# Another order of ScalarE's and VectorE's work inside a four-slot round of a fused decoder layer

## The chip, the core and the metric

The kernel runs on one NeuronCore of a Trainium2 chip. The metric is the device time of one execution in microseconds. The engines named below are TensorE (PE, with PEld for its weight loads), VectorE (DVE), ScalarE (ACT), GpSimd (POOL) and SyncE (SP, which only issues DMAs).

## The reference

One decoder layer with normalisation behind each residual, for 32 sequences of 256 tokens with 256 features:

```
x = layernorm(x + self_attention(x))
x = layernorm(x + cross_attention(x, ctx, cell))
x = layernorm(x + feed_forward(x))
```

- Self attention: 16 query heads of 64, 4 key/value heads, rotary positions, a linear position bias per head, a full softmax over 256 keys, output projection.
- Cross attention: layer norms with weights ahead of the q, k, v and output projections, 16 heads of 16, windows of 64 queries that look at their own and the previous window of keys, a mask by cell number, rotary positions.
- Feed forward: inner size 1024, `silu(gate) * up`, with weights rounded to -1, 0, 1 times a scale and activations rounded to 8 bits per row.

Inputs and outputs are float32; only the feed-forward products run in bfloat16, where the rounded values are exact.

## The kernel before

All 32 sequences ("batches") run in one unrolled program that is software-pipelined by hand. Time is cut into **slots**; a sequence takes 16 slots, four **rounds** of four slots (`part` 0 to 3). In round `m` the self attention works on pair `m` of units (a unit is 128 queries and two query heads per key/value head of a pair, 512 columns per tile), and the cross attention on unit `k = m - 4`, that is on the sequence before. The document calls the four rounds of a sequence A (slots 0 to 3), B (4 to 7), C (8 to 11) and D (12 to 15).

The order of instructions on TensorE, VectorE and ScalarE is the order in which the Python code calls them (`manual_schedule`). GpSimd and SyncE are not in that set: their instructions are ordered by the tile framework's planner, by its own estimate of when each becomes ready, and then run strictly in that order.

What one round does, by function and line:

- `self_scores` (line 393 on TensorE, 409 on VectorE): 8 matmuls into two banks `s`; then four VectorE instructions add the position bias, write `p` and give the negated row maximum `nm`. Two such units per round.
- `self_exp` (427, ScalarE): for each unit and half, two exponentials with their row sums.
- `self_values` (487 TensorE, 494 ScalarE): the previous pair's `pT` times `v` gives `o`; ScalarE copies it to `oT`. `self_normal` (500, VectorE) multiplies `oT` with `R`, the reciprocal sums.
- `cross_turn` (708 TensorE, 710 ScalarE): transposes the previous cross unit's exponentials `xp` and copies them to `xpT`, in two halves.
- `cross_scores` (669 TensorE, 683 VectorE), `cross_values` (724 TensorE, `xo`; 733 ScalarE, `xoT`), `cross_exp` (699 ScalarE, four exponentials per half).
- `self_inverse` (441, 443 VectorE, then a transposing DMA `planes`), and `self_spread` (455, GpSimd), which makes `R` of it.
- `self_turn` (470 TensorE, 475 ScalarE): transposes a unit's `p` and copies it to `pT`, two copies per unit.
- `cross_back` (744 TensorE, 749 and 750 VectorE): transposes the cross output back and divides it by its sums.

Between these, `parts()` runs the next step of every generator that is due in the slot: projections (`self_inputs`, 330, 339, 346; `cross_inputs`, 617, 629), output projections and norms (`self_output`, `cross_output`), and the feed forward. A generator's `yield n` says in how many slots it goes on. For example `self_output` starts in slot 9 (and 17): two steps of `wo` matmuls (508), the deferred normalisation (below) in slot 11 (19), the transposes `zqT` (204) with their copy `zT` (205, ScalarE) in slot 12 (20), and the `xq` matmuls (545) in slot 14 (22). Counted within a sequence's period of 16, the `zqT` steps fall into part 0 of rounds D and B. The other generators that run in part 0 have no ScalarE instruction in `parts()`.

A few instructions are deferred. A generator appends them to the list `last`, and `flush()` issues them at the end of the slot. Such are the normalisations `scaled` (198, ScalarE), and `residual` of `self_output`:

```
nc.vector.tensor_scalar(zq, h, mv[:, 0:1], rs[:, 1:2], ALU.subtract, ALU.mult)
nc.scalar.activation(x1, h, AF.Identity, bias=rs[:, 2:3], scale=rs[:, 0:1])
nc.gpsimd.tensor_tensor(x1, x1, xbias[O_], ALU.add)
```

What is appended in part 3: in slot 3 a `residual`; in slot 7 the two `scaled` of the context `cs`; in slot 11 another `residual`, the second `scaled` of the feed forward's output `y`, and the output DMA (194); in slot 15 nothing.

All TensorE outputs go through one pool of eight PSUM banks (`bank`, tag "b"), so a matmul group may wait until the engine that reads an older bank is done.

Of the kernel before, what the change touches and what calls it, by code (L numbers as in the profile page):

```python
# [51 lines left out]
def kernel(  # L52
# [139 lines left out]
    def flush():  # L192
        while last:
            last.pop(0)()
# [700 lines left out]
    with tc.manual_schedule(engines={mybir.EngineType.PE, mybir.EngineType.DVE, mybir.EngineType.Activation}):  # L895
        running = []
        slot = min(starts)
        while starts or running:
            m, part = divmod(slot, 4)
            k = m - CROSS  # L900
            for gen in starts.pop(slot, ()):
                running.append([slot, gen])

            def cross(f, unit, *more):
                if 0 <= unit < 4 * B:
                    f(*divmod(unit, 4), *more)

            def pair(f, unit):
                if 0 <= unit < 4 * B:
                    f(*divmod(unit, 4))  # L910

            def own(f, unit, *more):
                if 0 <= unit < 8 * B:
                    f(*divmod(unit, 8), *more)

            def parts():
                for r in list(running):
                    if r[0] == slot:
                        wait = next(r[1], r)
                        if wait is r:  # L920
                            running.remove(r)
                        else:
                            r[0] += wait or 1

            if part == 0:
                own(self_scores, 2 * m)
                own(self_scores, 2 * m + 1)
                own(self_exp, 2 * m, 0)
                own(self_exp, 2 * m, 1)
                own(self_exp, 2 * m + 1, 0)  # L930
                pair(self_values, m - 1)
                cross(cross_turn, k - 1, 0)
                cross(cross_turn, k - 1, 1)
                own(self_exp, 2 * m + 1, 1)
                parts()
                pair(self_normal, m - 1)
            elif part == 1:
                parts()
                cross(cross_scores, k)
                cross(cross_values, k - 1)  # L940
                cross(cross_exp, k, 0)
            elif part == 2:
                parts()
                pair(self_inverse, m)
                cross(cross_exp, k, 1)
                own(self_turn, 2 * m)
                cross(cross_back, k - 1)
            else:
                own(self_turn, 2 * m + 1)
                parts()  # L950
                pair(self_spread, m)
            flush()
            slot += 1

# [86 lines left out]
```

## Time and profile before

| | |
|---|---|
| median of 3 runs | 2209.35 us (2208.95 to 2211.95) |
| profiled execution | 2211.08 us, span of its trace 2209.3 us |
| mean granted TensorE clock | 0.98 |
| busy share PE, PEld | 95%, 73% |
| busy share DVE, ACT, POOL | 81%, 75%, 60% |
| DMA | 177.59 MB, mean 80 GB/s |

A profile line of a group reads: line, engine, operation, tiles written and read, count, busy time, mean duration in ns, idle time of the engine ahead of it and what ended that. A line of the list of waits reads: who waited, for whom, us in total, how many times, and the longest. A line of the timeline reads: start and duration in us, engine, line, operation, tiles, shapes, count, and in brackets the engine's idle time ahead of it with its releaser. A line of the windows reads: from and to, length, then busy time (and instruction count) of PE, PEld, DVE, ACT and POOL, the granted clock, DMA share and GB/s. The ends of matmuls are modelled, so the start-to-start distance of groups is the safer measure of TensorE.

### The profile page before, as it was taken

What the parts mean: (1) busy time and instruction counts of PE and PEld (TensorE: products, weight loads), DVE (VectorE), ACT (ScalarE), POOL (GpSimd) and SP (SyncE); (2) the same over time, 40 slices, a digit from 0 to 9 for tenths busy, and PEclk for the clock granted to TensorE, in tenths of its full rate; (3) what the DMA queues carried; (4) which work ended last, traced back from release to release, by engine and by line L of the source; (5) the groups of instructions that cost most, each with busy time, mean ns of one, the idle gap of its engine ahead of it and who ended that gap; (6) DMA issues with size and microseconds to landing.
All of it is one profiled execution on the core that took longest, in us unless ns stands there. A gap on an engine that the chain in (4) does not pass through costs nothing.

```text
span 2209.3 us, 54605 instructions
## 1 busy us (share of the span) xinstructions
PE 2103.3 (95%) x17254; PEld 1617.7 (73%) x17316; DVE 1789.9 (81%) x6949; ACT 1659.5 (75%) x4961; POOL 1316.8 (60%) x1977
## 2 busy tenths in 40 slices
PE   7899999999999999999999999999999999999984
PEld 5677777777777777777777777777777777777662
DVE  3877888888888888888888888888888888888775
ACT  2578778787778787778777778877777877777862
POOL 4465655666665666655656655656666556666542
PEclk8999999999999999999999999999999999999985
DMA  6433333333333334333333333334333333333221
GB/s 213 113 78 71 82 78 76 75 78 85 84 79 73 79 74 86 88 76 75 78 74 90 83 75 74 80 74 89 84 79 77 78 73 83 85 78 74 43 52 31
DMA packets 326592, 177.59 MB, mean 80 GB/s; under 512 B 242976, under 2 KB 296096, under 8 KB 326304
## 3 DMA queue, kind: packets, MB, share of 16 engines
q1 hardware_dynamic: 324608, 170.52, 34.1%
q10 hardware_dynamic: 1696, 3.57, 0.4%
q8 instruction: 138, 2.26, 0.4%
q14 instruction: 150, 1.23, 0.2%
HBM read 39.50 MB, written 8.39 MB: 22 GB/s over the span
## 4 chain that ended last, share of the span: by engine, by line
PE 58%; DVE 20%; ACT 12%; DMA 3%; issue 2%; POOL 1%; SPq 0%; ACTq 0%; POOLq 0%; DVEq 0%
PE wo L508 9%; PE t L470 8%; DVE p L409 7%; PE s L393 6%; ACT p L427 6%; PE o L487 5%; PE proj L330 5%; PE ff L811 4%; PE xq L545 3%; PE xt L708 3%; ACT xpT L710 3%; PE ffo L858 3%; PE xk L617 2%; PE xw L770 2%; PE v L362 2%; DMA out_dram<-x 2%
## 5 line engine op out<-in xcount | busy, mean ns | idle before, releaser
L427 ACT ACTIVATE p<-p,nm 128x256 f32<-128x256 f32 x1024 | 508.3, 499 | 235.8 <-DVE nm L409 235.8
L409 DVE CUSTOM_DVE_ANT_0 p<-s,alibi 128x256 f32<-128x256 f32 x1024 | 361.6, 416 | 3.2 <-PE s L393 3.2
L699 ACT ACTIVATE xp<-xp,xnm 128x128 f32<-128x128 f32 x1024 | 328.6, 401 | 47.0 <-DVE xnm L683 46.8
L393 PE MATMUL s<-kT,qT 64*128 64x256 f32 x2048 | 271.4, 392 | 0.0
L475 ACT COPY pT<-t 128x512 f32<-128x512 f32 x512 | 263.7, 598 | 7.0 <-PE t L470 6.8
L470 PE MATMUL t<-ident,p 128*128 128x128 f32 x2048 | 267.0, 273 | 0.9 <-ACT p L427 0.9
L354 POOL TENSOR_TENSOR qT<-qT,other 128x512 f32<-128x512 f32 x128 | 178.7, 1396 | 137.9 <-DMA other<-psin 113.1
L487 PE MATMUL o<-pT,v 128*64 128x256 f32 x2048 | 249.8, 386 | 0.0
L393 PEld LDWEIGHTS s<-kT,qT 64*128 64x128 f32 x2048 | 197.5, 187 | 68.6 <-issue 16.2
L330 PE MATMUL proj<-xT,wq_sb 128*128 128x256 f32 x1024 | 245.8, 384 | 0.0
L508 PE MATMUL wo<-wo_sb,oT 128*128 128x256 f32 x1024 | 244.1, 381 | 0.4 <-DVE oT L500 0.4
L470 PEld LDWEIGHTS t<-ident,p 128*128 128x128 f32 x2048 | 234.9, 142 | 9.4 <-ACT p L427 2.6
L683 DVE CUSTOM_DVE_ANT_0 xp<-xs,mask 128x128 f32<-128x128 f32 x1024 | 225.5, 284 | 13.2 <-PE xs L669 11.0
L508 PEld LDWEIGHTS wo<-wo_sb,oT 128*128 128x128 f32 x1024 | 192.9, 191 | 29.3 <-DVE oT L500 1.1
L487 PEld LDWEIGHTS o<-pT,v 128*64 128x64 f32 x2048 | 136.4, 137 | 98.1 <-issue 42.3
L330 PEld LDWEIGHTS proj<-xT,wq_sb 128*128 128x128 f32 x1024 | 187.7, 193 | 21.9 <-issue 0.4
L500 DVE TENSOR_TENSOR oT<-oT,R 128x512 f32<-128x512 f32 x128 | 98.0, 765 | 119.8 <-ACT oT L494 110.2
L427 ACT ACTIVATION_READ_ACCUMULATOR p<-p,nm 128x1 f32 x1024 | 194.1, 190 | 0.0
L455 POOL COPY R<-planes 128x1024 uint16<-128x1024 uint16 x128 | 173.5, 1356 | 21.9 <-DMA planes<-wide 21.6
L826 DVE SCALAR_TENSOR_TENSOR gu<-gu,ff 128x512 f32<-128x512 f32 x128 | 82.5, 684 | 100.7 <-ACT gu L825 100.6
L847 POOL TENSOR_SCALAR gu<-gu,ffhup 128x1024 f32<-128x1024 f32 x64 | 73.5, 1149 | 143.9 <-DVE ffhup L843 143.9
L708 PEld LDWEIGHTS xt<-ident,xp 128*128 128x128 f32 x1024 | 112.1, 143 | 49.0 <-issue 36.2
(147 smaller groups left out, 4530.8 us busy)
## 6 DMA issues: line engine op xcount, KB each, us to landing
other<-psin SPq DMA_DIRECT2D x640, 64.0 KB, 2.0
xT<-in_xt_dram SPq DMA_DIRECT2D x32, 256.0 KB, 2.8
xs<-in_x_dram SPq DMA_DIRECT2D x32, 256.0 KB, 2.7
cs<-in_ctx_dram SPq DMA_DIRECT2D x32, 256.0 KB, 2.8
other<-qb SPq DMA_DIRECT2D x64, 128.0 KB, 2.0
kTz<-tr SPq DMA_DIRECT2D x256, 32.0 KB, 2.0
other<-qb SPq DMA_DIRECT2D x128, 64.0 KB, 1.9
out_dram<-x SPq DMA_DIRECT2D x32, 256.0 KB, 2.4
```

The lines of the kernel that those rows point to most:

```text
L330: nc.tensor.matmul(pq[:, c * L : (c + 1) * L], w[:, dc, c * P : (c + 1) * P], xT[:, dc, :], start=(dc == 0), stop=(dc == NDC - 1),)
L354: nc.gpsimd.tensor_tensor(d2, d2, other, ALU.add)
L393: nc.tensor.matmul(banks[half][:, rr * L : (rr + 1) * L], qT[rows_, rr, qc * P : (qc + 1) * P], kT[rows_, kc, :], start=(rr == 0), stop=(r ...
L409: nc.vector.tensor_tensor_reduce(p[:, cols], banks[half][:, cols], alibi[:, 2 * (4 * kc + 2 * rp + rr) + half, :], -0.125, 3.0e38, ALU.add ...
L427: nc.scalar.activation(p[:, cols], p[:, cols], AF.Exp, bias=nm[:, rr : rr + 1], scale=-1.0, accum_out=s["sums", i // 2][:, e : e + 1],)
L470: nc.tensor.transpose(pt[:, j * P : (j + 1) * P], p[half][:, rr * L + kk * P : rr * L + (kk + 1) * P], ident,)
L475: nc.scalar.copy(pT[half], pt)
L487: nc.tensor.matmul(po[half * HD : (half + 1) * HD, rp * L : (rp + 1) * L], s["v"][:, kk, (2 * kc + half) * HD : (2 * kc + half + 1) * HD], ...
L508: nc.tensor.matmul(py[:, 0:D], s["oT", qc, kc][:, r, :], wo_sb[:, 4 * kc + r, :], start=(kc == 0 and r == 0), stop=(kc == 1 and r == 3),)
L683: nc.vector.tensor_tensor_reduce(p[:, cols], banks[2 * half + j // 2][:, j % 2 * P : (j % 2 + 1) * P], s["mask"][:, qc, :], -1.0, 3.0e38, ...
L699: nc.scalar.activation(p[:, cols], p[:, cols], AF.Exp, bias=s["xnm", i][half][:, j : j + 1], scale=-1.0)
L708: nc.tensor.transpose(pt[:, j * P : (j + 1) * P], p[:, j * P : (j + 1) * P], ident)
```

## The change

The diff moves calls inside the round's four parts. In part 0 the second unit's scores are issued behind the first unit's exponentials and a new `flush()`; the generators' steps run ahead of the second unit's last exponentials. The two halves of the cross exponentials move from part 1 and the head of part 2 to behind the first unit's transposes (part 2) and behind the generators' steps of part 3. The `flush()` at the end of part 3 is left out: what part 3 deferred is issued by the flush in the next part 0, or behind the loop for the last slot.

```
             if part == 0:
                 own(self_scores, 2 * m)
-                own(self_scores, 2 * m + 1)
                 own(self_exp, 2 * m, 0)
                 own(self_exp, 2 * m, 1)
+                flush()
+                own(self_scores, 2 * m + 1)
                 own(self_exp, 2 * m + 1, 0)
                 pair(self_values, m - 1)
                 cross(cross_turn, k - 1, 0)
                 cross(cross_turn, k - 1, 1)
+                parts()
                 own(self_exp, 2 * m + 1, 1)
-                parts()
                 pair(self_normal, m - 1)
             elif part == 1:
                 parts()
                 cross(cross_scores, k)
                 cross(cross_values, k - 1)
-                cross(cross_exp, k, 0)
             elif part == 2:
                 parts()
                 pair(self_inverse, m)
-                cross(cross_exp, k, 1)
                 own(self_turn, 2 * m)
+                cross(cross_exp, k, 0)
                 cross(cross_back, k - 1)
             else:
                 own(self_turn, 2 * m + 1)
                 parts()
+                cross(cross_exp, k, 1)
                 pair(self_spread, m)
-            flush()
+            if part < 3:
+                flush()
             slot += 1
+        flush()
```

The order of the calls that issue TensorE instructions stays as it was: `self_scores` of both units, `self_values`, `cross_turn`, the generators.

More of the change, by code (lines that the diff above doesn't have):

```diff
@@ L926 @@
                 own(self_scores, 2 * m)
-                own(self_scores, 2 * m + 1)
                 own(self_exp, 2 * m, 0)
                 own(self_exp, 2 * m, 1)
+                flush()
+                own(self_scores, 2 * m + 1)
                 own(self_exp, 2 * m + 1, 0)
@@ L933 @@
                 cross(cross_turn, k - 1, 1)
+                parts()
                 own(self_exp, 2 * m + 1, 1)
-                parts()
                 pair(self_normal, m - 1)
@@ L940 @@
                 cross(cross_values, k - 1)
-                cross(cross_exp, k, 0)
             elif part == 2:
@@ L944 @@
                 pair(self_inverse, m)
-                cross(cross_exp, k, 1)
                 own(self_turn, 2 * m)
+                cross(cross_exp, k, 0)
                 cross(cross_back, k - 1)
@@ L950 @@
                 parts()
+                cross(cross_exp, k, 1)
                 pair(self_spread, m)
-            flush()
+            if part < 3:
+                flush()
             slot += 1
+        flush()
 def shape_constants():
```

## The prediction

> **What bounds the kernel now.** I read the page first, then the windows, the list of waits, and last the timeline of one batch. Batches repeat every 65.5 to 66 us, so one is enough.
>
> ```profile
> PE 2103.3 (95%) x17254; PEld 1617.7 (73%) x17316; DVE 1789.9 (81%) x6949; ACT 1659.5 (75%) x4961; POOL 1316.8 (60%) x1977
> ```
> ```profile
> 60.00:1000.00 940.00, 914.68 (x7563) 708.53 (x7585) 778.13 (x3018) 728.77 (x2195) 572.13 (x838) 1.00 0.36 81
> ```
>
> The second line is the steady state by window (PE, PEld, DVE, ACT, POOL, clock): TensorE has a matmul in flight for 914.7 of 940 us at full clock. It is the bound, and all that an order of instructions can win is its waits.
>
> Here a rule of the Trainium skill speaks against the change: "Perfetto Trace Analysis", Identifying the Most-Contended Engine, holds matmul occupancy to be no measure of headroom and asks for weight-load occupancy (here 73%), while for VectorE occupancy is fair. By it VectorE (81%) is the most contended, the diff takes none of its 1790 us away, and the sum would be 0. The row I follow is the spacing of matmul starts: `proj` x8 in 1.8 us, `t` x8 in 0.87, with nothing between groups except at four places per batch. Those places lose about 2.4 of 65.8 us, so a perfect order gains 75 us at most, and the rule's 27% isn't there.
>
> ```profile
> ACT p L427 <- DVE nm L409: 235.8, 94, 21.9
> DVE oT L500 <- ACT oT L494: 110.2, 120, 2.8
> ACT cs L198 <- POOL rstd_zc L186: 84.1, 33, 6.8
> PE xq L545 <- ACT zT L205: 37.8, 61, 0.8
> PEld s L393 <- ACT pT L475: 16.0, 59, 0.4
> ```
>
> The fourth line is TensorE's only large wait: `xq` waits for ScalarE's copy of `zqT`, 61 times. The fifth: `s` waits for a bank that ScalarE's copies of `pT` release. The first three are idle time of engines that is harmless now and decides what the moves cost.
>
> I call the four pairs of a batch A (slots 0 to 3), B, C and D; each starts at its first `s`: D at 1118.8, A at 1132.94, B at 1147.60, C at 1162.81. D and A in the timeline (start, duration):
>
> ```profile
> 1120.90 0.81 DVE L533 TENSOR_SCALAR row<-row,mv_x,rs_x 128x256 f32<-128x256 f32 x1
> 1122.14 0.51 ACT L427 ACTIVATE p<-p,nm 128x256 f32<-128x256 f32 x1 [4.65 <-DVE nm L409]
> 1125.11 0.56 ACT L494 COPY oT<-o 128x512 f32<-128x512 f32 x1
> 1125.58 1.06 ACT L710 COPY xpT<-xt 128x512 f32<-128x512 f32 x2
> 1126.33 0.79 PE L724 MATMUL xo<-xpT,xvaug 128*32 128x64 f32 x32
> 1126.53 0.52 ACT L427 ACTIVATE p<-p,nm 128x256 f32<-128x256 f32 x1
> 1127.53 0.36 ACT L205 COPY zT<-zqT 128x256 f32<-128x256 f32 x1
> 1127.94 1.16 PE L545 MATMUL xq<-zT,xq_w 128*128 128x128 f32 x8 [0.82 <-ACT zT L205]
> ...
> 1132.94 2.49 PE L393 MATMUL s<-kT,qT 64*128 64x256 f32 x16
> ...
> 1137.17 0.51 ACT L427 ACTIVATE p<-p,nm 128x256 f32<-128x256 f32 x1 [1.18 <-DVE nm L409]
> ...
> 1141.49 0.65 PE L724 MATMUL xo<-xpT,xvaug 128*32 128x64 f32 x32
> ...
> 1142.08 1.04 PE L811 MATMUL ff<-ff_up,xiT 128*128 128x512 bf16 x3
> ```
>
> An unhindered `xo` x32 takes 0.59 us (1141.49 to 1142.08). In D it takes 1.61 (1126.33 to 1127.94): 1.02 lost. In B (xo 1155.02, xq 1156.08, nominal 0.57) 0.48 is lost. In A, `s` x16 takes 2.49 instead of 2.00: 0.49 lost. D loses 0.2 to 0.8 more at `xs` and `xo`, behind the copies of `oT` and `xpT`.
>
> **The change part by part.** No instruction is added or removed; ScalarE and VectorE get another order, TensorE keeps its own. Durations from rows: exponential 0.495 start to start, `oT` 0.47, two `xpT` 0.96, two `pT` 1.02, four cross exponentials 1.18, a scaled copy 0.50, `zT` 0.25.
>
> *Parts ahead of the last two exponentials.* `zT` is a part of slot 12 (D) and slot 4 (B). It passes two exponentials, 0.99 us. The other part-0 slots have no ScalarE part.
>
> *Flush between the self units.* Part 3 of slots 3, 7, 11 leaves deferred work: for B `zq` (VectorE, line 533) and `x1`; for C two `cs`; for D the last `y`, its output DMA, `zq` and `x1`. Before, `zq` stood ahead of all eight biases (L409); now only ahead of the second four, so the first exponential comes 0.74 earlier (1120.90 against 1121.63 in D, 1149.03 against 1149.77 in B). In return ScalarE's items, which filled idle time (the 4.65 us ahead of 1122.14), stand in its busy chain.
> - D: exponentials from 1121.41; four, 1.97; `y` and `x1`, 1.00; two, 0.99: `oT` at 1125.37 (+0.26), `xpT` 1125.84 to 1126.90, `zT` 1126.79 to 1127.15 instead of 1127.89. `xo`'s second half needs the second `xpT` and ends about 1127.2; `xq` starts there: gain 0.7. `zq` now ends about 1123.1, before `zqT` at 1123.43; this cover is 0.3 us, beyond it each tenth delays `zqT`, but `xo` waits anyhow.
> - B: the cross exponentials end near 1149.6, so exponentials start there; four, `x1`, two, `oT`, `xpT` make 4.89: `zT` ends 1154.85, `xq` follows `xo` at 1155.6. Gain 0.48, all of its wait.
> - C: two `cs` (1.0) between the exponentials; they had stood ahead of them, waiting 2.3 us for POOL. B's gain moves C's `s` 0.48 nearer to a VectorE that is busy without a gap from 1153.9 on. The `zcT` copies slip from 1172.4 to about 1173.4; they release the bank that `xo` (1173.89) seems to take. Loss between 0 and 0.4; I take 0.1, since `xo` started on time in nine batches of ten. `oT` on VectorE is 0.9 later and is absorbed by its 2.1 us wait for `wo` (L518).
>
> *Cross exponentials behind the copies.* Both sets move behind `pT` of their slot, 1.2 to 2.4 us of ScalarE work, so `pT` of the first unit leaves before A's `s`: the 0.49 at `s` goes. But ScalarE then runs without a pause from D's exponentials to A's: my sum of its rows (8 self exponentials, y, x1, oT, xpT, zT, on, xoT, qb, tanh x4, zT, pT x4, 8 cross) is 15.0 us, so the last cross exponentials end 4.1 us into A, as A's biases arrive (1137.17 is 4.23). `xt` needs them at 4.25. A's `xpT` is then ready 8.6 us into A and `xo`, which would come at 8.07, ends at 9.0 instead of 9.15: of 0.49 only 0.15 stays.
>
> *SP and POOL* have no written order; their queues follow the planner. Issues keep their number. The output DMA now waits for a `y` some 7 us later; `R` (L455) and `x1`+bias (L535) may change places on POOL. I cost both at nothing in the likeliest case: kept apart below.
>
> Sum: D 0.7, A 0.15, B 0.48, C -0.1: 1.2 us a batch. About 30 of 32 batches are full: 36 us; head and tail, where engines wait for DMAs, I leave at 0 (each within 2). Span 2209.3 - 36 = 2173.3; the profiled execution has 1.8 outside it (2211.1) and lies 1.7 above the median, so the median becomes **2173**.
>
> **The rivals.**
> 1. *Slower: the output DMA blocks SP.* Now it is issued at 1117.04, followed at once by `planes` (1117.54), the `psin` swaps, `xvaug` and `xiT` (1122.78). Its `y` will end about 5.3 us into D. If it keeps its place, all those wait: `xiT`, behind 5 us of issues, comes at D+10.5 instead of D+4.0 and lands past D+13; the gate matmuls want it at D+9.6. 3.5 us lost, less the 1.2 gained, 30 times: +69, **2278**. For it: SP is strictly in order. Against: the planner placed this DMA right behind its `y` now (SP 1117.04, y ended just before), so it should move. It decides once `xiT` is more than about 3 us late (2 of slack and the gain). Chance 0.16.
> 2. *The gain moves to the next wait.* ScalarE has no slack left from D to A; if its semaphores or `xs` (bank behind `oT`, now +0.26) add 0.3 in each of D and A, only B and a little remain: 0.6 a batch, **2191**. For it: the 0.26 is certain. Against: `xq` was far behind in D. Chance 0.20.
> 3. *POOL puts x1+bias ahead of R in B.* It then waits for `x1` (2.9 us later than now); `R` ends 1.3 later than VectorE's `oT` needs, VectorE carries it into C, `xo` there loses about 1.0: **2203**, no measurable gain or little. For it: L535 precedes R now. Against: R's planes have landed by then. Chance 0.12.
>
> **How the numbers follow.** The likeliest has 0.52, and alone 2160 to 2188 (0.7 to 1.65 us a batch: C's loss from 0 to 0.4, A's gain from 0 to 0.49). Reaching to cases 2 and 3 gives 2160 to 2214, which leaves out case 1 and a little below. What can be told from no change is about 0.2%, 4.4 us (2205 to 2214). Faster: 0.52, 0.20 and a third of case 3's edge: 0.73. Same: most of case 3, 0.09. Slower: 0.18.
>
> **What would show it.** `PE xq <- ACT zT` falls from 37.8 us to under 8; `PEld s <- ACT pT` nearly goes; `ACT cs <- POOL rstd_zc` goes; `s` x16 in A takes 2.0; batches repeat every 64.4 to 64.9 us. ScalarE's idle time ahead of A's exponentials (1.18) goes to about 0. Wrong, if `PE xo` or `xs` waits for `xpT` and `oT` by more than was won, if gate matmuls wait for `xiT`, or if `DVE oT` waits for POOL's `R`.

## The result and the profile after

The changed kernel takes **2210.62 us** (median of 12, 2207.43 to 2214.73) against 2210.39 (2208.95 to 2212.15) for the kernel before, measured side by side: ratio 1.0001, 95% interval 0.9992 to 1.001. No change; 2173 was predicted. Its profiled span is 2211.5 us, before 2209.3.

First the busy times on the page of the changed kernel:

```profile
PE 2126.2 (96%) x17316; PEld 1612.2 (73%) x17316; DVE 1811.3 (82%) x6949; ACT 1662.3 (75%) x4961; POOL 1333.6 (60%) x1977
```

TensorE shows 23 us more than before for the same matmuls in the same order (the page before has 62 fewer records of them). This says nothing of the time: matmuls that wait can be counted as busy. Of the versions below, `bc` needs 2102.5 busy us for the same 17316 matmuls, and b_only shows 2.79 us of work for sixteen `s` that take 2.00 unhindered.

The list of waits of the changed kernel (engine and line, what it waited for, us in all, times, longest):

```profile
ACT p L427 <- DVE nm L409: 224.6, 67, 21.8
DVE oT L500 <- ACT oT L494: 123.3, 114, 2.9
...
PEld xo L724 <- ACT xpT L710: 23.2, 59, 1.7
...
PEld wo L508 <- ACT oT L494: 15.9, 28, 1.0
...
PEld xs L669 <- ACT oT L494: 11.7, 28, 0.5
...
PEld s L393 <- ACT pT L475: 9.6, 29, 0.3
...
PE wo L508 <- ACT oT L494: 8.3, 18, 0.7
```

All three waits that the change aimed at are gone or smaller: TensorE's `xq` for `zT` (37.8 us) and `cs` for `rstd_zc` (84.1) are no longer in the answer, and `s` for `pT` fell from 16.0 to 9.6. But `wo` (L508) now waits for ScalarE's `oT`, once in nearly every batch; this line was not there before.

Where the time went is seen from the four rounds of a batch, each from its first `s` to that of the next round. The table gives their mean length over 27 batches, read from the start times in the timeline. The versions in its lower rows are explained below.

| us | A | B | C | D | batch |
|---|---|---|---|---|---|
| before | 14.67 | 15.21 | 21.56 | 14.37 | 65.82 |
| after | 14.87 | 14.73 | 22.23 | 14.10 | 65.92 |
| expected gain of after | 0.15 | 0.48 | -0.1 | 0.7 | 1.23 |
| measured gain of after | -0.20 | 0.48 | -0.67 | 0.27 | -0.10 |
| b_only | 14.98 | 14.73 | 21.64 | 14.11 | 65.45 |
| c_only | 14.29 | 15.04 | 21.61 | 14.39 | 65.34 |
| a_only | 14.74 | 14.96 | 21.84 | 14.88 | 66.42 |
| bc | 14.91 | 14.72 | 21.67 | 13.53 | 64.83 |
| bc_nokeys | 14.42 | 14.73 | 21.67 | 13.55 | 64.37 |
| bc_kp2 | 14.42 | 14.72 | 21.63 | 13.55 | 64.32 |

B came out to the hundredth. Against the forecast A lost 0.35 us, C 0.57 and D 0.43. Each loss can be followed in the timeline.

**Round A** of the changed kernel, one that begins at 1199.34 (start, duration, engine):

```profile
1199.34 2.00 PE L393 MATMUL s<-kT,qT 64*128 64x256 f32 x16
1199.62 1.42 SPq L653 DMA_DIRECT2D kTz<-tr  x2
1201.15 2.23 SPq L448 DMA_TRANSPOSE planes<-wide  x1
1203.43 3.23 SPq L653 DMA_DIRECT2D kTz<-tr  x5
1206.28 0.56 ACT L494 COPY oT<-o 128x512 f32<-128x512 f32 x1
1206.76 0.78 PE L669 MATMUL xs<-kTz,xqT 32*128 32x256 f32 x6
1208.17 0.66 PE L669 MATMUL xs<-kTz,xqT 32*128 32x256 f32 x2 [0.63 <-DMA kTz<-tr]
1208.77 0.65 PE L724 MATMUL xo<-xpT,xvaug 128*32 128x64 f32 x32
```

`s` takes 2.00 as forecast. `xs` begins 7.42 us into A (before, 7.91), does six of its eight matmuls, and waits for the last keys: `kTz` is filled by eight small DMAs, the last is issued at 1206.1 and lands 2.0 us later, just ahead of the last two matmuls. SP issues almost without a gap from 1194.6 until then; the five keys at the end come every 0.65 us. Before, the last key landed 7.1 us into A on average (6.4 to 8.0), ahead of `xs`; after, on average at 8.0.

**Round C** of the changed kernel, beginning at 1097.06, and then of the kernel before, beginning at 1162.81:

```profile
1101.88 0.51 ACT L427 ACTIVATE p<-p,nm 128x256 f32<-128x256 f32 x1 [3.49 <-DVE nm L409]
...
1103.86 1.07 ACT L198 ACTIVATE cs<-cs,rstd_zc 128x256 f32<-128x256 f32 x2
...
1105.83 0.56 ACT L494 COPY oT<-o 128x512 f32<-128x512 f32 x1
...
1106.44 1.99 PE L508 MATMUL wo<-wo_sb,oT 128*128 128x256 f32 x8 [0.58 <-ACT oT L494]
1106.49 0.97 DVE L500 TENSOR_TENSOR oT<-oT,R 128x512 f32<-128x512 f32 x1 [1.29 <-ACT oT L494]
...
1108.98 0.64 PE L724 MATMUL xo<-xpT,xvaug 128*32 128x128 f32 x16
```
```profile
1167.00 0.50 ACT L427 ACTIVATE p<-p,nm 128x256 f32<-128x256 f32 x1
...
1169.95 0.56 ACT L494 COPY oT<-o 128x512 f32<-128x512 f32 x1
...
1171.45 1.89 PE L508 MATMUL wo<-wo_sb,oT 128*128 128x256 f32 x8
...
1173.89 0.64 PE L724 MATMUL xo<-xpT,xvaug 128*32 128x128 f32 x16
```

From the start of the round, the exponentials begin at 4.82 (before 4.19), `oT` is copied at 8.77 (7.14): 0.63 from the later `nm`, and 1.0 from the two `cs` that now stand among the exponentials. `wo` begins at 9.38 (8.64), `xo` at 11.92 (11.08). The `wo` of this round multiplies an older `oT`; what it wants is the PSUM bank that ScalarE's copy releases (in the order of the calls, its bank is the eighth that is taken after that of `o`, from a pool of eight).

**Round D** gets this lateness through VectorE, SP and POOL. POOL at the end of C and in D (D begins at 1119.41), then the same before (D begins at 1118.81). The batch of the changed kernel is one of its later ones:

```profile
1114.76 1.27 POOL L354 TENSOR_TENSOR qT<-qT,other 128x512 f32<-128x512 f32 x1 [4.88 <-DVE row L518]
...
1118.53 0.73 POOL L525 TENSOR_TENSOR rs_x<-rs_x,neg_half 128x2 f32<-128x2 f32 x1
...
1119.60 0.94 POOL L798 TENSOR_SCALAR tr<-x,ffup 128x256 f32<-128x256 f32 x2
1120.51 1.27 POOL L579 TENSOR_TENSOR qb<-qb,rx_sb 128x512 f32<-128x512 f32 x1
1120.58 1.48 DVE L800 TENSOR_SCALAR xib<-tr 128x512 bf16<-128x512 f32 x1 [0.30 <-POOL tr L798]
...
1122.53 0.39 DVE L409 CUSTOM_DVE_ANT_0 p<-s,alibi 128x256 f32<-128x256 f32 x1
```
```profile
1116.31 1.36 POOL L798 TENSOR_SCALAR tr<-x,ffup 128x256 f32<-128x256 f32 x2
1117.64 1.27 POOL L579 TENSOR_TENSOR qb<-qb,rx_sb 128x512 f32<-128x512 f32 x1
...
1119.59 0.84 DVE L800 TENSOR_SCALAR xib<-tr 128x512 bf16<-128x512 f32 x1
```

`oT` on VectorE (L500) begins 9.26 into C on average (8.06), the second `psin` (L339) at 11.58 (9.86), its swaps on SP at 12.33 (10.61), and `tr` (L798) on POOL at 21.41 (19.74). In this D, `xib` waits for POOL's `tr` and then runs beside POOL's rotation of K: 1.48 us instead of 0.84. VectorE's first bias, which the change was to bring 0.74 us forward, comes 3.12 us into this D, later than the 2.82 of the batch shown before. Over the 27 batches the effect is smaller: `xib` begins late in only three of them, it lasts 1.25 us on average (1.07), and the first bias comes at 2.56 (3.07). So 0.51 of the 0.74 us arrived.

### The profile page after: what moved, and what is told of

The parts are those of the page before. It is cut to its first block, busy times and chain, and to the rows that moved or that the text cites. A ratio compares the mean times of both kernels' runs of the same rounds, so it can differ in the third digit from the quotient of the medians.

```text
span 2211.5 us, 54581 instructions
## 1 busy us (share of the span) xinstructions
PE 2126.2 (96%) x17316; PEld 1612.2 (73%) x17316; DVE 1811.3 (82%) x6949; ACT 1662.3 (75%) x4961; POOL 1333.6 (60%) x1977
## 4 chain that ended last, share of the span: by engine, by line
PE 60%; DVE 12%; ACT 10%; POOL 7%; DMA 5%; issue 4%; SPq 1%; ACTq 0%; POOLq 0%; DVEq 0%
PE wo L508 9%; PE t L470 7%; PE s L393 6%; PE o L487 6%; PE proj L330 5%; PE ff L811 5%; PE xs L669 4%; ACT p L427 4%; PE xt L708 3%; PE xo L724 3%; PE xq L545 2%; PE xk L617 2%; DVE p L409 2%; PE xv L629 2%; PE ffo L858 2%
## 5 line engine op out<-in xcount | busy, mean ns | idle before, releaser
L475 ACT COPY pT<-t 128x512 f32<-128x512 f32 x512 | 276.5, 601 | 64.6 <-PE t L470 64.2
L354 POOL TENSOR_TENSOR qT<-qT,other 128x512 f32<-128x512 f32 x128 | 165.4, 1292 | 163.8 <-DMA other<-psin 158.5
L393 PE MATMUL s<-kT,qT 64*128 64x256 f32 x2048 | 258.3, 392 | 0.0
L508 PE MATMUL wo<-wo_sb,oT 128*128 128x256 f32 x1024 | 247.8, 385 | 10.2 <-ACT oT L494 8.3
L393 PEld LDWEIGHTS s<-kT,qT 64*128 64x128 f32 x2048 | 188.7, 188 | 63.8 <-DVE on L750 12.3
L500 DVE TENSOR_TENSOR oT<-oT,R 128x512 f32<-128x512 f32 x128 | 118.1, 923 | 138.4 <-ACT oT L494 123.3
L508 PEld LDWEIGHTS wo<-wo_sb,oT 128*128 128x128 f32 x1024 | 193.7, 192 | 45.9 <-ACT oT L494 15.9
L708 PE MATMUL xt<-ident,xp 128*128 128x128 f32 x1024 | 143.0, 280 | 2.1 <-ACT xp L699 2.1
```

What stands on the lines that cost most here:

```text
L393: nc.tensor.matmul(banks[half][:, rr * L : (rr + 1) * L], qT[rows_, rr, qc * P : (qc + 1) * P], kT[rows_, kc, :], start=(rr == 0), stop=(r ...
L475: nc.scalar.copy(pT[half], pt)
L508: nc.tensor.matmul(py[:, 0:D], s["oT", qc, kc][:, r, :], wo_sb[:, 4 * kc + r, :], start=(kc == 0 and r == 0), stop=(kc == 1 and r == 3),)
L708: nc.tensor.transpose(pt[:, j * P : (j + 1) * P], p[:, j * P : (j + 1) * P], ident)
```

## The experiments

The three parts of the change are called b (`parts()` ahead of the last two self exponentials), c (cross exponentials behind the copies) and a (the deferred work of part 3 of slots 3, 7 and 11 between the next two self units). Three theories follow from the rows above. **First:** the deferred work, once among the self exponentials, makes ScalarE's `oT` late in C, and VectorE and POOL carry it into D. **Second:** ScalarE has no slack from D to A, so what is won in D comes back in A. **Third:** with A's `s` on time, the next limit of A are the keys, which SP issues late. The rival to all three is that a move is worth nothing wherever it is put. Every version was timed beside the kernel before (2209.4 to 2213.0 us there); ratios are to it.

**b alone.**

```
+                parts()
                 own(self_exp, 2 * m + 1, 1)
-                parts()
```

> Only the generators' steps move ahead of the last two self exponentials. Theory 1 (local): zT is 0.99 us earlier, the wait of xq goes in B (0.48) and D (about 0.9), nothing is lost elsewhere: 1.4 us a batch, time about 2168. Theory 2 (ScalarE's chain): the work that ScalarE does from D's exponentials to A's has no pause, so what D wins comes back in A, whose biases wait for the tanh of the gate; only B's 0.48 stays: about 2196. Theory 3 (the key DMAs): with D 0.9 shorter the masked key tile kTz lands later in A and xs waits for it; same total as theory 2, but A's xs is split by a wait instead of A's biases being late.

2200.24 us, ratio 0.9948 (0.9936 to 0.9961). B keeps its 0.48: b alone gives all of it. D gains only 0.26 and A loses 0.31, as the second theory says. In D the wait at `xq` is gone, but the gate matmuls now wait for `gu`, which waits for ScalarE's tanh; this line of b_only's list of waits is in neither of the two kernels':

```profile
PE ff L811 <- DVE gu L826: 12.5, 30, 0.4
```

A of b_only:

```profile
1129.44 2.79 PE L393 MATMUL s<-kT,qT 64*128 64x256 f32 x16
1129.59 2.06 ACT L475 COPY pT<-t 128x512 f32<-128x512 f32 x4
```

`s` x16 takes 2.79 here (2.49 before): the four `pT` copies that release its banks end at 1131.65, two microseconds into the round.

**c alone.**

```
                 cross(cross_values, k - 1)
-                cross(cross_exp, k, 0)
...
-                cross(cross_exp, k, 1)
                 own(self_turn, 2 * m)
+                cross(cross_exp, k, 0)
...
                 parts()
+                cross(cross_exp, k, 1)
```

> Only the cross exponentials move behind the copies of pT. Theory 1: the wait of s in A (0.49) goes and A's exponentials come 0.5 to 0.9 us earlier relative to A, xo follows, 0.4 us a batch: about 2197; B, C and D as before. Theory 3 (keys): kTz lands 7.0 to 7.5 us into A and A's xs now wants it at 7.7, so little of it is lost. If A stays at 14.7, the gain is taken by xs or xo and the wait before it tells by what.

2202.38 us, ratio 0.9957 (0.9945 to 0.997). A falls by 0.38, D keeps its wait at `xq`.

**a alone.**

```
                 own(self_scores, 2 * m)
-                own(self_scores, 2 * m + 1)
                 own(self_exp, 2 * m, 0)
                 own(self_exp, 2 * m, 1)
+                flush()
+                own(self_scores, 2 * m + 1)
...
-            flush()
+            if part < 3:
+                flush()
...
+        flush()
```

> Only the normalisations deferred in part 3 move between the self units. Theory 1 (what the trace of the changed kernel shows): in C the two cs put the copy of oT 0.7 us later and wo waits for its bank, C about 0.5 longer; in D y and x1 put zT 0.3 later, D 0.3 longer; in B zT is 0.24 earlier, B 0.24 shorter: 0.5 us a batch lost, about 2226. Rival (this part is what makes the rest work, since it brings the biases forward 0.74 us): 2209 or below.

2226.33 us, ratio 1.0072 (1.0058 to 1.0086). It is slower by itself, by the sum expected but not by its shares: C +0.28, D +0.51. It does shorten B by 0.25, but b has all of B's gain without it.

**b and c together.**

> The changed kernel with the flush of part 3 at its old place. Theory 1: B 0.48 and D 0.7 shorter, A's s wait gone, C as before; held in A by ScalarE and the keys: 0.9 to 1.3 us a batch, 2170 to 2182. Rival: the loss does not lie in the moved flush, and this runs as the changed kernel does, 2205 to 2215.

**2183.22 us**, ratio 0.9877 (0.9859 to 0.9895). Together they win more (27 us) than the two alone (21): `zT` early in D needs the `pT` copies early at D's end, or A takes the gain back. The busy times on the page of bc, and its list of waits:

```profile
PE 2102.5 (97%) x17316; PEld 1609.5 (74%) x17316; DVE 1768.7 (81%) x6949; ACT 1660.7 (76%) x4961; POOL 1320.0 (61%) x1977
```
```profile
PEld s L393 <- ACT pT L475: 9.6, 29, 0.3
...
PEld xs L669 <- ACT oT L494: 7.8, 14, 1.1
```

`s` waits as little as in the whole change, and no wait of `wo` for ScalarE's `oT` stands in this answer. D is 13.53, a gain of 0.84. A stays at 14.91, with keys landing 7.3 to 8.7 us into it. So part a costs 27 us on top of b and c.

**Which slot's deferred work costs.** Three versions, each an edit of the changed kernel:

```
-            if part < 3:
+            if slot % 16 not in (3, 11):   # after_keep7: slot 7's work stays in its slot
+            if slot % 16 != 11:            # bc_move11: of part a, only slot 11's work moves
+            if slot % 16 != 7:             # bc_move7: only slot 7's work moves
                 flush()
```

> The changed kernel, but the flush of slot 7 (the two cs) stays at the end of its slot. Theory: the two cs put the copy of oT behind the moment at which wo wants its bank, so C falls from 22.2 to 21.6 with D and A as they were: 2211 - 17 = 2194. Rival: C's extra length comes from B's gain (VectorE reaches C late), then C stays at 22.1 and the time at 2208 or above.

2187.09 us, ratio 0.9896 (0.9882 to 0.9909): 23 us won back, more than the 17 expected. They don't all lie in C: its mean falls only to 21.87, since two batches of three run it in 21.5 as before and every third takes 22.4 to 23.0. D falls from 14.10 to 13.75, its first bias comes at 2.32, and A falls to 14.76.

> The parts and the cross exponentials moved, and of the deferred work only slot 11's (y, x1, zq, output DMA) moved between the self units. Theory: y and x1 stand in D's busy chain on ScalarE, D goes from 13.53 back to 14.1 while B and C stay at 14.72 and 21.65: 2183 + 17 = 2200. Rival: the moved zq brings D's biases 0.7 forward and balances it, 2180 to 2186.

2192.75 us, ratio 0.9922 (0.9909 to 0.9936). Between the two numbers expected: slot 11's move costs some 10 us of bc's gain, with C 21.90 (again every third batch) and D 13.76. In D the rows show why: the first bias comes 0.8 us earlier than in bc, but `y` and `x1` put 1.0 us among the exponentials, so ScalarE copies `oT` 0.16 us later (6.75 against 6.59).

> The first two parts of the change and of the third only slot 7 (two scaled copies between the self exponentials of C). If slot 7's move is what costs (the whole change without it is 23 us better), this is 2200 to 2208, with C near 22.2 and D a few tenths longer than 13.53. If the 23 us came only with slot 3's and 11's moves, 2181 to 2190.

2198.69 us, ratio 0.9937 (0.9925 to 0.995): 13 to 15 us, a little under the range given, with C 22.17 as expected. The costs don't add up exactly (13 and 10 alone, 23 for slot 7 where the others are moved too), but slot 7 is the dearer each time. Slot 3's move was not made alone; bc_move11 and after_keep7 differ by it, and the one that has it is the faster by some 6 us, at the edge of what can be told apart. The first theory holds: two `cs` of 0.5 us at the wrong place are the largest single loss.

**The keys.** In the three versions that follow, the loads of `kTz` are left out for all but the first two sequences, so cross attention works with old keys.

```
+                if b < 2:
+                    nc.sync.dma_start(kTz[rows_, :, j, :], kT[rows_, :, :])
-                nc.sync.dma_start(kTz[rows_, :, j, :], kT[rows_, :, :])
```

> The changed kernel, with the eight key DMAs (kTz, line 653) left out for all sequences but the first two, so that their cross attention uses old keys; xs still runs. Theory 3 (keys): in A the fourth row group of xs starts 0.14 us after the last kTz lands, 0.3 to 1.2 us late; without it A falls from 14.87 to 14.3 or 14.4 and the time by 13 to 17 us, to about 2196. Theory 2 (ScalarE's chain holds xo in A): xpT is ready no earlier, A stays within 0.15 of 14.87, time 2206 or above.

2192.52 us, ratio 0.9916 (0.9903 to 0.993): 18 us; A falls from 14.87 to 14.27. The trace of the changed kernel alone would not have told this size: of the waits at `xs` (L669) it puts only 3.3 us, six times, down to the key DMAs.

> The kernel before with the loads of the padded cross keys (kTz) left out for all but the first two sequences, so that cross attention uses old keys. Control. If the keys became a limit only because the change makes round A earlier (before, they landed 0.4 to 1.4 us ahead of xs), leaving them out is worth nothing here: 2205 to 2213. If the five issues cost SP time that other transfers wait for, it gains by itself: 2195 or less, and the 18 us seen with the change are not the keys' lateness alone.

2211.05 us, ratio 0.9995 (0.9987 to 1.0003). In the kernel before, the same loads cost nothing.

> The first two parts of the change, deferred work left where it was, and the key loads left out as in the control. If round A of this version (14.91 us) is held by the last key load alone, A falls to about 14.3 and the time to 2163 to 2168 (0.6 us times 30 less than 2183). If ScalarE's chain from D to A holds it as well, A stays above 14.6 and the time above 2174.

2167.53 us, ratio 0.9798 (0.9785 to 0.9812): A 14.42. The third theory holds, and only for a kernel in which A has become earlier.

**Why the keys are late.** A second tile was to show whether they wait for their tile or for SP.

```
+    kTz_bufs = [ctile([P, NDC, 2, L], F32, f"kTz{i}") for i in range(2)]
...
-        yield 3
+        yield 1               # bc_keys3: yield 3
+        kTz = kTz_bufs[b % 2]
...
 # to make room, in both: psin 2 buffers instead of 3, row 3 instead of 4
```

> The parts and the cross exponentials moved, the flush as before, and two key tiles kTz in turn, filled two slots earlier in the order (for their room psin has two buffers and row three). Theory 3 (keys): A falls from 14.93 to about 14.4, nothing else changes: 2183 - 16 = 2167. Rival: the earlier key DMAs push the psin swaps, planes or xiT back on SP, and another wait takes the place: 2180 or above.

2312.79 us, ratio 1.0459 (1.0442 to 1.0476).

> The first two parts of the change, with two tiles for the padded keys in turn, filled at the same point of the order as before (and psin and row with one buffer less, to make room). If the keys come late because their tile is still being read by the sequence before, they now land earlier and the time is 2165 to 2175. If they come late because SP reaches their issues late (0.65 us each, behind those of D), a second tile gives nothing: 2180 to 2190, or more if the buffers taken from psin and row are missed.

2302.29 us, ratio 1.0407 (1.039 to 1.0425), outside both of its ranges unless the missing buffers count. SP's issues of bc_keys3 in D, which begins at 1161.45, then a line of SP's own waits, then some of the other waits:

```profile
1165.62 0.70 SPq L655 DMA_DIRECT2D kTz<-tr  x1
1166.41 2.48 SPq L313 DMA_DIRECT2D other<-psin  x4
...
1170.29 3.39 SPq L807 DMA_TRANSPOSE xiT<-xib  x2
```
```profile
SPq L655 <- POOL tr L582: 120.5, 30, 5.4
```
```profile
POOL qT L355 <- DMA other<-psin: 256.0, 82, 8.0
DVE oT L501 <- POOL R L456: 130.0, 33, 5.6
...
PEld L814 <- DMA xiT<-xib: 54.7, 32, 6.9
```

With a second tile the planner puts the first key issue ahead of `psin`'s swaps, and so ahead of POOL's rotation of the keys (`tr`, L582), which that issue needs. SP's queue stands until the rotation is done: 4 us in each of 30 batches (in bc this wait occurs once, 3.0 us). The swaps come 5.0 us into D instead of at its start, and `xiT` 8.8 us into D instead of 3.7. POOL waits 256 us for the swaps (113 in bc), and the gate matmuls wait for `xiT` in every batch. A batch is 3.9 us longer than in bc, as much as the queue stands. bc_keys2 has the same wait, 116.5 us. Both versions changed two things, so the buffers were taken away alone:

> The first two parts of the change with one tile for the keys, and psin and row with one buffer less, as in the two versions with two key tiles. If the missing buffers made those versions slow (POOL's qT waited 256 us in all for psin's swaps), this is 2285 to 2315. If the second key tile did it, by earlier issues that push others back, this stays at 2180 to 2195.

2185.31 us, ratio 0.9884 (0.9871 to 0.9898): the buffers cost nothing. This leaves the order of SP's queue for the loss of 120 to 130 us; no run put the first key issue back behind its data with two tiles. Then the issues were taken off SP, the tile left as it is:

```
-                nc.sync.dma_start(kTz[rows_, :, j, :], kT[rows_, :, :])
+                nc.gpsimd.dma_start(kTz[rows_, :, j, :], kT[rows_, :, :])   # bc_kpool
+                nc.scalar.dma_start(kTz[rows_, :, j, :], kT[rows_, :, :])   # bc_kact
```

> The first two parts of the change, with the eight key loads issued by POOL instead of SP. If SP's full queue from D to A is what makes the keys late, A falls from 14.9 to about 14.4 us and the time to 2165 to 2175, as long as POOL, 60% busy, can carry the issues. If POOL's own chain (its K rotation and R) is delayed by the issues, DVE oT waits for POOL R by more and the time is 2185 to 2220.

2186.42 us, ratio 0.9887 (0.9874 to 0.9901). The keys now land 3.5 to 5.6 us into A, some 3 us before `xs`. So the tile is free in time (POOL waits for its readers 9.6 us in all), and SP's queue made the keys late. Yet A is 14.85. bc_kpool's list of waits:

```profile
DVE oT L500 <- POOL R L455: 45.4, 28, 4.8
...
PEld wo L508 <- DVE oT L500: 20.0, 28, 1.9
```

In bc these waits are 8.2 and 1.2 us. Eight issues of 0.5 us on POOL push its `R` behind the point where VectorE wants it, and `wo` waits for VectorE.

> The same with the eight key loads issued by ScalarE. If SP's queue makes the keys late and an issue costs ScalarE little, 2165 to 2175. If each issue holds ScalarE for some 0.6 us as it holds SP, round D or A pays up to 5 us of ScalarE's chain a batch: 2230 to 2330.

2338.99 us, ratio 1.0581 (1.0566 to 1.0595); A 20.12, 5.2 us longer. One row of the view of L653 in bc_kact (count, and ns min/median/max of one):

```profile
L653 ACTq DMA_DIRECT2D kTz<-tr x256: 592/605/2241, 83.1 to 2239.4; - x128
```

Eight times 0.61 us is 4.9 us of ScalarE's chain: the second theory once more, from the other side. Last, the issues were shared:

```
+                (nc.gpsimd if r >= 3 else nc.sync).dma_start(kTz[rows_, :, j, :], kT[rows_, :, :])   # bc_kp4: r >= 2
```

> The first two parts of the change, with two of the eight key loads issued by POOL and six by SP. On SP the last key then lands about 1.3 us sooner (7.4 at the latest instead of 8.7), and POOL carries 1.0 us more instead of 4.0. If both queues have that much to spare, A is 14.4 to 14.6 and the time 2168 to 2175. If POOL has nothing to spare, R is late already and the time is 2180 to 2190.

**2172.56 us**, ratio 0.982 (0.9805 to 0.9835).

> The same with four key loads on POOL and four on SP: keys at about 6 us, POOL 2.0 us more. If POOL's slack ends between 2 and 4 us, 2166 to 2174; if it ends below 2, 2176 to 2190, worse than with two.

2174.77 us, ratio 0.9827 (0.9813 to 0.9841). With two or with four on POOL, A is 14.42, as short as without any key loads. The two can't be told apart. bc_kp2's busy times and its waits:

```profile
PE 2095.3 (97%) x17316; PEld 1605.4 (74%) x17316; DVE 1766.8 (82%) x6949; ACT 1660.7 (77%) x4961; POOL 1355.7 (63%) x2041
```
```profile
DVE oT L500 <- POOL R L455: 8.5, 4, 4.4
```

It computes all that the kernel before does and takes 1.8% less time; the changed kernel is as slow as the one before.

## Why the prediction was wrong

- **Bound and scale: right.** TensorE's waits were the whole prize. The best version won 39 us of the 75 that the spacing of the matmuls allowed, with no instruction fewer than before. The sum of 0 that I set against it was my own inference: the section cited in the prediction (the Trainium skill, "Perfetto Trace Analysis", Identifying the Most-Contended Engine) says which engine to optimise first. It does not say that an order of instructions can win nothing.
- **B, 0.48: right in size, partly by luck.** I gave it to the early `nm` and the early `zT` together. b_only shows that `parts()` alone does it.
- **C, -0.1: the step that failed first.** It read "`oT` on VectorE is 0.9 later and is absorbed by its 2.1 us wait for `wo`". The wait was there, but `wo` itself moved: it needs the bank that ScalarE's copy of `oT` releases. For `xo` I had asked which copy releases its bank; for `wo` I followed only the readers of the data. C lost 0.67. Slot 7's move alone makes bc's C 0.50 longer; with only slot 7's work left in its slot, C falls from 22.23 to 21.87, and two batches of three are back at 21.5.
- **D, 0.7: the mechanism was right, the undisturbed round was not what D got.** With slot 7's work left in its slot, the first bias comes 0.75 us earlier (I had 0.74) and D gains 0.62. In the whole change POOL comes 1.7 us later out of C, the first bias is only 0.51 earlier, and 0.27 is left. My step "SP and POOL ... I cost both at nothing" named two items and missed POOL's `tr` and SP's `psin` swaps. And the part that brings the biases forward does not pay in D at all: b and c without it give 0.84.
- **A, 0.15: the mechanism at `s` was right, the next limit was not named.** I had ScalarE's `xpT` as the limit of `xo`. It was the last key DMA, ahead of it, in no step of mine. The old trace held it: the last key landed 0.85 us before `xs` on average, and `xs` was to come 0.5 us earlier in a round that itself began earlier against SP's queue. Measured -0.20; without the keys +0.40.
- **Rivals.** The output DMA moved behind `xiT` (issued 6 to 7 us into D), so rival 1 did not happen; bc_keys2 and bc_keys3 show its mechanism with another DMA, an issue that waits for its data and holds up SP's queue. In B, POOL put `R` ahead of `x1`+bias, so rival 3 did not happen. Rival 2, the gain moving to the next wait, is what happened in A, but at the keys and not at `xs` and `xo` behind `oT`: 18 us. The 23 us of slot 7's `cs` are no rival's; they belong to step C. So the time lies inside the range given, near rival 3's number, by a path that I had not priced.

What is not settled: why slot 11's move makes C longer in every third batch, why the costs of the slots don't add up, and what slot 3's move is worth alone.

## What to carry to other kernels

When an engine is to start earlier, list everything that it reads, DMAs too, with the time by which each lands ahead of it now; the smallest of these bounds what the move can win as long as they stay where they are. A key DMA that a list of waits hardly shows was worth 18 us. When an instruction of another engine is delayed, ask who uses its source bank next, not only who reads its result. Test the parts of a combined change one by one: here two parts won 1.2% and the third lost just that.

## What the runs showed of the hardware

- The issue of one 32 KB key DMA occupied SP's queue for 0.59 us and came every 0.65 us in a row of five; it occupied ScalarE for 0.61 us and POOL for 0.50 (medians of after, bc_kact and bc_kpool). Eight of them on ScalarE lengthened round A by 5.2 us; with two or four of them on POOL, A was as short as without any.
- One issue on SP that stood ahead of its data held up those behind it for 4 us a batch (120.5 us in 30 waits, bc_keys3).
- A matmul group (`wo`) that read nothing of a ScalarE copy began 0.05 us after that copy ended, 0.74 us late, because the copy read the PSUM bank that the group was to write (C of the changed kernel).
- `xib` (L800, VectorE, 128x512 to bf16) takes between 0.43 and 1.58 us; its mean is 1.04 before and 1.18 after. The long one shown here lies beside POOL's `qb` (L579). That POOL's work is the cause was not tested by itself.
